# A graph network on one core: edge rows copied to PSUM by ScalarE in the first pass, row ends found tile by tile instead of by counting, and a longer ring of gathered rows

## The chip, the core and the metric

The kernel runs on one core of a Trainium2 chip. A time is the device time of one execution, in microseconds. The kernel before has the median, the lowest and the highest of three runs. The profile is one further execution, recorded by the hardware profiler. TensorE is called PE in the profile, VectorE DVE, ScalarE ACT, GpSimd POOL and SyncE SP.

## The reference

There are N = 6,250 nodes with 256 features and E = 100,000 edges, sorted by their destination `dst`; an edge also has 64 attributes. Two layers of message passing follow one another:

```
theta_x = (x[dst] - x[src]) @ theta_w.T + theta_b
phi_x   = x[src] @ phi_w.T + phi_b
x = layernorm(x + where(isfinite(m), m, 0)),  m = segment_max(relu(theta_x + phi_x), dst)

hv = x @ W_in + b_in
for W, b in ((W_u0, b_u0), (W_u1, b_u1)):
    msg = segment_max(relu(concat(hv[src], edge_attr) @ W + b), dst)
    hv  = where(has_in, msg + hv, hv)          # has_in: the node has an incoming edge
x = layernorm(x + relu(hv @ W_ro + b_ro))
```

All data are 32-bit floats. The relu and the terms of the destination don't depend on the choice of the edge, so they can be applied after the maximum: for the first layer the kernel needs the segment maximum of `x[src] @ (phi - theta)` alone, and for the other two rounds that of `hv[src] @ W[:256] + edge_attr @ W[256:]`.

## The kernel before

**Three passes.** `sweep(r)` runs three times, r = 0 for the first layer and r = 1, 2 for the two rounds of the second. Each pass reads a table in device memory, `table[r]`, with one row of 256 numbers a node: `table[0]` is `x @ (phi - theta)`, made in the prologue; pass 0 writes `table[1]` and pass 1 writes `table[2]`, a tile of 128 nodes at a time. There are 49 such tiles.

**Edges, blocks and steps.** The edges are laid out in reverse order of `dst`, in 14 blocks: 13 of 128 x 56 edges and a last of 128 x 54. Partition p of a block holds 56 consecutive edges. A step takes one edge of each partition, so a pass has 782 steps. Eight steps make a group (`K`).

**One step.** POOL gathers the 128 rows of the step's sources by an indirect DMA into `run`, a ring of groups (`sources`, line 790). It is issued `AHEAD` = 16 steps before the step, and the ring has four groups. DVE then keeps a running maximum along each partition (line 1043): the new value is `max(min(previous, lim), row)`, where `lim` is very low at the first edge of a node, so that the maximum starts anew there. The result replaces the gathered row. In passes 1 and 2 PE first multiplies the edge attributes of two steps (`pair`, line 825, into one of three PSUM buffers of the tag `he`, two pairs ahead), and DVE adds the gathered rows of both steps to it (line 1030). In pass 0 DVE takes the rows from SBUF as they were gathered. Forty steps of pass 0, the first two of each of the first 20 groups, are "raw": their rows are gathered from `x` itself, before the table is complete, then transposed and multiplied on PE (`raw_turn`, `raw_pair`).

**Behind the steps.** When a group is done SP stores it to `S[r]` (line 1051, 1 MB). At the end of a block `over_lanes` carries maxima over from partition to partition: PE transposes the last column, DVE scans it, PE transposes back, and ACT copies the result to `cs` (line 857).

**Node tiles.** `node(t, g, b)` puts the work of a tile of 128 nodes at slots, numbers of steps. At slot g POOL gathers the row of each node's last edge from S into `m` (line 870), which waits for the stores of S made so far. At b - 3 and b - 2 the maxima carried into the tile's partitions are picked by a matmul (`picks`, `carried`). In pass 0 follow `first_a` to `first_g`, from b to b + 9: the maximum with the carried one, adding theta of the node (from `h_sb`), relu times `has` on ACT (line 909), adding x, layernorm, two transposes (line 760), a copy by ACT (line 762), a product with `wcat` (line 768), the row for `table[1]` (line 926) and `h_sb`. In passes 1 and 2, `next_a` (lines 931 and 932) to `next_d` or `last_g` do the like with the next weights.

**Theta.** In pass 0, `theta(x)` of one tile each eight steps is made from a transposed copy of x, loaded by SP (lines 894, 897, 900).

**Counting.** The position of a node's last edge (`end_i`) and whether it has one (`has`) come from a count of edges by node, made in pass 0: `count(c)`, 98 times, one group each three steps from slot 28. DVE builds one-hot rows of the low 7 bits (`ol`, line 710) and of the tile number (`oh`, line 716), and PE adds up their products (line 721). At slots 322 and 323 `ends_a` and `ends_b` sum the counts. So no node tile of pass 0 starts before slot 324 (`begin`), which is in the sixth block.

**What sets the order.** The schedule is by hand. The loop over steps issues, for each step, a gather for 16 steps later, the pair two pairs ahead, DVE's work, the store, and then the tasks that `at(slot, ...)` has put there. Each engine works through its instructions in just this order, and waits on semaphores for operands and for free buffers. `node`'s slots are chosen at the end of `sweep`: b is at least `gap` slots (6, 4 and 6 in the three passes) after the tile before, and about 20 slots after the end of the last block that holds edges of the tile. `ahead` and `sources_next` gather the first 24 steps of the next pass while the present one ends.

A branch in `gnn_kernel` leads to `any_order`, for edges that are not sorted or lie otherwise than the blocks expect. It isn't taken with these inputs.

Of the kernel before, what the change touches and what calls it, by code (L numbers as in the profile page):

```python
# [8 lines left out]
F32 = mybir.dt.float32  # L9
# [14 lines left out]
K = 8  # L24
# [24 lines left out]
AHEAD = 2 * K  # L49
# [15 lines left out]
WIDE = max(sum(a <= b <= z for a, z in SPAN) for b in range(NB))  # L65

# [7 lines left out]
def gather_raw(nc, x, x_sb, s_r, i):  # L74

    nc.gpsimd.indirect_dma_start(out=x_sb[:, i, :], out_offset=None, in_=x,
                                 in_offset=bass.IndirectOffsetOnAxis(ap=s_r[:, i:i + 1], axis=0))
# [382 lines left out]
def gnn_kernel(  # L460
# [13 lines left out]
    above = const.tile([P, P], F32)  # L474
    nc.vector.tensor_scalar(above, jmp, 0.0, None, OP.is_gt)
# [4 lines left out]
    col = const.tile([P, P], BF16)  # L480
    nc.vector.tensor_copy(col, col_i)
# [22 lines left out]
    wd = const.tile([P, 2, D], F32)  # L504
    wt = const.tile([P, 2, D], F32)
# [6 lines left out]
    lo = const.tile([P, FS], BF16)  # L512
    hi = const.tile([P, FS], BF16)
    with tc.manual_schedule(), tc.tile_pool(name="pro", bufs=2) as pro, \
# [6 lines left out]
        for i in range(SOON):  # L521
            gather_raw(nc, x, x_sb, s_r, i)
        zero = pro.tile([1, D], F32, name="zero", bufs=1)
# [14 lines left out]
        def check():  # L538
# [15 lines left out]
            alike = BLOCKS.count(BLOCKS[0])  # L554
# [9 lines left out]
            nc.vector.tensor_scalar(bits, d_s, P - 1, None, OP.bitwise_and)  # L564
            nc.vector.tensor_copy(lo, bits)
            nc.vector.tensor_scalar(bits, d_s, 7, None, OP.arith_shift_right)
            nc.vector.tensor_copy(hi, bits)
# [29 lines left out]
def in_order(ctx: ExitStack, tc: tile.TileContext, g):  # L597
# [9 lines left out]
    table, ident, above, every, col, col_f = (g[n] for n in ("table", "ident", "above", "every", "col", "col_f"))  # L607
    whole, lim, lo, hi, s_s, fd, pd, ld, nd = (g[n] for n in ("whole", "lim", "lo", "hi", "s_s", "fd", "pd", "ld", "nd"))
    heT, xTn, xn, out = (g[n] for n in ("heT", "xTn", "xn", "out"))
    s_e, head, x, x_sb, wd, s_r = (g[n] for n in ("s_e", "head", "x", "x_sb", "wd", "s_r"))  # L610
    part = g["part"]
# [6 lines left out]
    has = one.tile([P, NT], F32, name="has")  # L618
# [3 lines left out]
    ones = one.tile([P, NT], F32, name="ones")  # L622
    nc.vector.memset(ones, 1.0)
# [18 lines left out]
    wcat = one.tile([P, 2, 2 * D], F32, name="wcat")  # L642
    nc.scalar.dma_start(wcat[:, :, :D], g["w_in"].rearrange("(k p) f -> p k f", p=P))
    winT = weight(g["w_inT"], "winT")
    wu0 = weight(g["w_u0"][:D, :], "wu0")
# [50 lines left out]
    hist = psum.tile([P, 512], F32, tag="v", name="hist", bufs=1)  # L696

    none = one.tile([P, NT], BF16, name="none")
    nc.vector.memset(none, 0.0)
    half = (NG + 1) // 2  # L700
    low = []
    for i in range(2):
        low.append(psum.tile([P, 512], F32, tag="he", name="low", bufs=3))
        n = min(half * K, FS - i * half * K)
        nc.scalar.copy(low[i][:, :n], lo[:, i * half * K:i * half * K + n])

    def count(c):
        k = min(K, FS - c * K)
        ol = work.tile([P, K, P], BF16, name="ol", bufs=1)
        nc.vector.tensor_tensor(ol[:, :k, :], col.unsqueeze(1).to_broadcast([P, k, P]),  # L710
                                low[c // half][:, c % half * K:c % half * K + k].unsqueeze(2).to_broadcast([P, k, P]), OP.is_equal)
        b = max(i for i in range(NB) if FIRST[i] <= c * K)
        tiles = [t for t in range(NT) if SPAN[t][0] <= b <= SPAN[t][1]]
        t0, w = tiles[0], len(tiles)
        oh = work.tile([P, K, WIDE], BF16, name="oh", bufs=1)
        nc.vector.tensor_tensor(oh[:, :k, :w], col[:, t0:t0 + w].unsqueeze(1).to_broadcast([P, k, w]),  # L716
                                hi[:, c * K:c * K + k].unsqueeze(2).to_broadcast([P, k, w]), OP.is_equal)
        if c == 0:
            nc.tensor.matmul(hist[:, :NT], ol[:, 0, :], none, start=True, stop=False)
        for j in range(k):  # L720
            nc.tensor.matmul(hist[:, t0:t0 + w], ol[:, j, :], oh[:, j, :w], start=False,  # L721
                             stop=(c == NG - 1 and j == k - 1))

    cnt, incl, end = (one.tile([P, NT], F32, name=n) for n in ("cnt", "incl", "end"))
    sums = []

    def ends_a():
        nc.vector.tensor_copy(cnt, hist[:, :NT])
        ps = psum.tile([P, 512], F32, tag="pr", name="sums")
        nc.tensor.matmul(ps[:, :NT], above, cnt, start=True, stop=True)  # L730
        nc.tensor.matmul(ps[:, 64:64 + NT], every, cnt, start=True, stop=True)
        sums.append(ps)
        nc.vector.tensor_scalar(has, cnt, 0.0, None, OP.is_gt)

    def ends_b():
        lower, total = sums[0][:, :NT], sums[0][:, 64:64 + NT]
        nc.vector.tensor_tensor_scan(incl, ones, total, 0.0, OP.mult, OP.add)
        nc.vector.tensor_sub(end, total, incl)
        nc.vector.tensor_sub(end, end, lower)
        nc.vector.tensor_add(end, end, has)  # L740
        nc.vector.tensor_scalar(end, end, float(E - 2), 0.0, OP.add, OP.max)
        nc.vector.tensor_copy(end_i, end)
# [22 lines left out]
    def times(aT, w, n, tag="pr"):  # L765
        ps = psum.tile([P, 512], F32, tag=tag, name="prod", bufs=3 if tag == "he" else 2)
        for k in range(2):
            nc.tensor.matmul(ps[:, :n], aT[:, k, :], w[:, k, :], start=(k == 0), stop=(k == 1))  # L768
        return ps

    def sweep(r):
# [12 lines left out]
        def sources(s, r=r, runs=runs):  # L784
            if s % K == 0:
                runs[s // K] = work.tile([P, K, D], F32, name="run", bufs=4)
# [7 lines left out]
        def raw_turn(i):  # L794

            tp = psum.tile([P, 512], F32, tag="tp", name="tp")
            for q in range(4):
                nc.tensor.transpose(tp[:, q * P:(q + 1) * P], x_sb[:, 2 * i + q // 2, q % 2 * P:(q % 2 + 1) * P], ident)
            rT[i] = work.tile([P, K // 2, P], F32, tag="hT", name="rT", bufs=4)
            nc.scalar.copy(rT[i].rearrange("p k e -> p (k e)"), tp)  # L800

        def raw_pair(i):
            aT = rT.pop(i)
            hp[i * K // 2] = psum.tile([P, 512], F32, tag="pr", name="hp")
            for q in range(4):
                nc.tensor.matmul(hp[i * K // 2][:, q // 2 * D:(q // 2 + 1) * D], aT[:, q, :], wd[:, q % 2, :],
# [26 lines left out]
        def over_lanes(b, last):  # L833
# [18 lines left out]
            def back():  # L852
# [4 lines left out]
                nc.scalar.copy(cs[:, b % KEPT, :D], cp[:, :D])  # L857
# [4 lines left out]
        def node(t, g, b):  # L862
# [5 lines left out]
            def rows():  # L868
                o["m"] = work.tile([P, D], F32, name="m", bufs=7)
# [8 lines left out]
            def picks():  # L878
                o["pick"] = []
                for blk in range(SPAN[t][0], SPAN[t][1] + 1):  # L880
                    p = work.tile([P, P], F32, name="pick", bufs=4)
# [10 lines left out]
            def x_in():  # L892
                o["xT"] = work.tile([P, K // 2, P], F32, tag="hT", name="xT", bufs=4)[:, :2, :]
                nc.sync.dma_start(o["xT"], xTn[:, :, t * P:(t + 1) * P])

            def theta():
                o["h"] = times(o["xT"], th, D, tag="he")

            def theta_out():
# [219 lines left out]
```

## Time and profile before

| what | us |
|---|---|
| runs: median (lowest to highest of three) | 4056.26 (4050.23 to 4058.96) |
| profiled execution | 4011.58 |
| its span | 4009.8 |
| pass 0, first to last step on DVE | 99.1 to 1366.2 |
| pass 1 | 1395.1 to 2678.2 |
| pass 2 | 2700.2 to 3994.0 |
| busy: PE, DVE, ACT, POOL | 1862.9, 2118.4, 238.2, 2391.0 |
| mean granted clock of TensorE | 0.689 |

"Busy" is the time in which an engine works on an instruction; an engine that waits for a semaphore isn't busy. In a row of groups, the numbers are: line, engine and operation, output and inputs by their names, sizes, count; busy time in us and mean of one in ns; the idle time just before these instructions, with what ended most of it. In a row of waits they are: the engine, the tile and line that waited, what it waited for, the total in us, how often, and the longest. "Issue" means that nothing in the trace shows a wait; "remote" is a semaphore whose event can't be told.

### The profile page before, as it was taken

How to read it: one execution, taken by the hardware profiler on the slowest of the kernel's cores; microseconds unless marked ns; L12 is line 12 of the kernel's file. 1: busy time of each engine (PE TensorE's matmuls, PEld its weight loads, DVE VectorE, ACT ScalarE, POOL GpSimd, SP SyncE). 2: the span in 40 equal slices, each digit the busy share in tenths (PEclk: the TensorE clock that was granted, in tenths of full speed). 3: DMA queues.
4: the chain of work that ended last, by engine and by line, in shares of the span. 5: the costliest groups of instructions: out<-in, count | busy, mean ns of one | idle time of the engine just before them, and what ended most of it. 6: DMA issues, size and time to landing. Idle time of an engine off the chain costs nothing. (4 is left out here: it accounts for less than half of the span.)

```text
span 4009.8 us, 21650 instructions
## 1 busy us (share of the span) xinstructions
PE 1862.9 (46%) x4631; PEld 825.8 (21%) x4631; DVE 2118.4 (53%) x4750; ACT 238.2 (6%) x618; POOL 2391.0 (60%) x2500
## 2 busy tenths in 40 slices
PE   5552123545520255454545555545544454444555
PEld 4341111212210122221112211111222221111111
DVE  1476444545543365554455555545756655555555
ACT  1000000111100000000000000000000000000000
POOL 5456546665667656656565656565655556666663
PEclk8665555766555578777676777667877777777766
DMA  6456545554555566555555556555555555555554
GB/s 235 149 197 231 171 140 178 188 165 165 177 193 169 178 198 203 185 178 185 170 182 187 192 197 207 185 175 192 194 181 179 183 181 189 182 182 193 186 194 161
DMA packets 241821, 739.39 MB, mean 184 GB/s; under 512 B 52485, under 2 KB 95858, under 8 KB 204434
## 3 DMA queue, kind: packets, MB, share of 16 engines
q0 software_dynamic: 119664, 326.92, 27.6%
q1 hardware_dynamic: 69568, 337.85, 22.6%
q10 hardware_dynamic: 52450, 73.16, 5.6%
q14 instruction: 100, 0.82, 0.1%
q8 instruction: 39, 0.64, 0.1%
HBM read 404.56 MB, written 333.17 MB: 184 GB/s over the span
## 5 line engine op out<-in xcount | busy, mean ns | idle before, releaser
L790 POOL DMA_INDIRECT run<-table,s_s x2258 | 2163.4, 958 | 1254.2 <-issue 666.1
L825 PE MATMUL hp<-whe,hT 128*128 128x512 f32 x1564 | 1015.0, 746 | 823.7 <-DVE run L1043 487.2
L1043 DVE SCALAR_TENSOR_TENSOR run<-run,lim,hp 128x256 f32<-128x256 f32 x1573 | 753.8, 479 | 55.7 <-issue 9.1
L1030 DVE TENSOR_TENSOR hp<-hp,run 128x512 f32<-128x512 f32 x782 | 543.2, 695 | 377.7 <-remote 196.2
L825 PEld LDWEIGHTS hp<-whe,hT 128*128 128x128 f32 x1564 | 300.8, 224 | 1369.8 <-DVE run L1043 815.7
L1043 DVE SCALAR_TENSOR_TENSOR run<-run,lim 128x256 f32<-128x256 f32 x731 | 351.5, 481 | 148.7 <-remote 56.0
L870 POOL DMA_INDIRECT m<-S,end_i x147 | 141.4, 962 | 304.5 <-DMA S<-run 177.0
L889 PE MATMUL v<-cs,pick 128*128 128x256 f32 (+1 forms) x438 | 167.0, 501 | 164.3 <-issue 71.0
L768 PE MATMUL prod<-wcat,aT 128*128 128x512 f32 x196 | 172.1, 1029 | 56.9 <-issue 34.0
L931 DVE TENSOR_TENSOR m<-m,v 128x256 f32<-128x256 f32 x98 | 40.6, 414 | 296.6 <-remote 232.1
L710 DVE TENSOR_TENSOR ol<-col,low 128x1024 bf16<-128x1024 bf16 x98 | 118.9, 1213 | 118.3 <-remote 103.9
L721 PE MATMUL hist<-oh,ol 128*128 128x8 bf16 (+7 forms) x782 | 34.9, 167 | 289.2 <-DVE oh L716 210.6
L889 PEld LDWEIGHTS v<-cs,pick 128*128 128x128 f32 x438 | 102.2, 253 | 270.4 <-issue 213.6
L768 PE MATMUL prod<-wro,aT 128*128 128x256 f32 x196 | 80.0, 548 | 166.0 <-issue 94.9
L947 DVE TENSOR_TENSOR m<-prod,bro 128x256 f32<-128x256 f32 x49 | 20.8, 425 | 233.0 <-remote 66.4
L768 PE MATMUL prod<-wu,aT 128*128 128x256 f32 x196 | 69.2, 486 | 91.2 <-issue 68.7
L926 DVE TENSOR_TENSOR new<-prod,b 128x256 f32<-128x256 f32 x49 | 20.8, 424 | 165.5 <-PE prod L768 67.3
L760 PE MATMUL tp<-ident,x_sb 128*128 128x128 f32 x98 | 31.8, 425 | 153.8 <-DVE x_sb L755 76.4
L721 PEld LDWEIGHTS <-ol 128*128 128x128 bf16 x782 | 36.4, 104 | 315.0 <-DVE ol L710 225.7
L932 ACT ACTIVATE m<-m,has 128x256 f32<-128x256 f32 x98 | 49.7, 508 | 858.8 <-DVE m L931 381.9
L760 PE MATMUL tp<-ident,h_sb 128*128 128x128 f32 x196 | 48.9, 338 | 110.9 <-DVE h_sb L935 52.0
L762 ACT COPY aT<-tp 128x256 f32<-128x256 f32 x147 | 54.8, 373 | 699.3 <-remote 292.7
(131 smaller groups left out, 1389.9 us busy)
## 6 DMA issues: line engine op xcount, KB each, us to landing
S<-run SPq DMA_DIRECT2D x291, 1024.0 KB
hT<-in_heT ACTq DMA_DIRECT2D x196, 256.0 KB
run<-table,s_s POOLq DMA_INDIRECT x2258
table<-new ACTq DMA_DIRECT2D x98, 128.0 KB
xg<-in_xTn SPq DMA_DIRECT2D x7, 896.0 KB
xT<-in_xTn SPq DMA_DIRECT2D x49, 128.0 KB
x_sb<-in_xn SPq DMA_DIRECT2D x7, 896.0 KB
out<-new ACTq DMA_DIRECT2D x48, 128.0 KB
```

What stands on the lines that cost most here:

```text
L710: nc.vector.tensor_tensor(ol[:, :k, :], col.unsqueeze(1).to_broadcast([P, k, P]), low[c // half][:, c % half * K:c % half * K + k].unsquee ...
L721: nc.tensor.matmul(hist[:, t0:t0 + w], ol[:, j, :], oh[:, j, :w], start=False, stop=(c == NG - 1 and j == k - 1))
L760: nc.tensor.transpose(tp[:, k * P:(k + 1) * P], a[:, k * P:(k + 1) * P], ident)
L762: nc.scalar.copy(aT.rearrange("p k e -> p (k e)"), tp[:, :2 * P])
L768: nc.tensor.matmul(ps[:, :n], aT[:, k, :], w[:, k, :], start=(k == 0), stop=(k == 1))
L790: nc.gpsimd.indirect_dma_start(out=runs[s // K][:, s % K, :], out_offset=None, in_=table[r][:SPARE + 1, :] if early else table[r], in_offs ...
L825: nc.tensor.matmul(hp[i], hT[c][:, q, :], whe[r - 1].rearrange("p s f -> p (s f)"), start=True, stop=not early)
L870: i = nc.gpsimd.indirect_dma_start(out=o["m"], out_offset=None, in_=S_r[:P * (FIRST[SPAN[t][1]] + BLOCKS[SPAN[t][1]]), :], in_offset=bass. ...
L889: nc.tensor.matmul(o["v"][:, :N1], p, cs[:, blk % KEPT, :N1], start=(blk == SPAN[t][0]), stop=(blk == SPAN[t][1]))
L932: nc.scalar.activation(o["m"], o["m"], AF.Relu, scale=has[:, t:t + 1])
L1030: nc.vector.tensor_add(sums, sums, two)
L1043: nc.vector.scalar_tensor_tensor(cur, prev, lim[:, s:s + 1], row, OP.min, OP.max)
```

## The change

- `AHEAD` is 24 steps, and the ring of `run` has five groups. In passes 1 and 2 every sixth group takes the place of three weights, `wd`, `wt` and `wcat`, which only the prologue and pass 0 use and which now lie together in `first_w`.
- To find room, `m` has five buffers instead of seven, and `winT` and `wu0` are loaded into tiles of `hT`'s ring.
- The counting is gone, with its one-hots, `ends_a`, `ends_b` and `begin`. In its place, `ends(t)` finds the last edges of one tile twelve slots before they are gathered: for each block that the tile spans, two operations mark the partition whose run holds a node's last edge, a matmul picks that partition's list of destinations, and DVE counts along it. `keeps` takes the place of `has`: very high where a node has an edge and very low where not.
- Node tiles of pass 0 therefore start after the first block, 8 slots apart instead of 6.
- In pass 0 all rows reach DVE through PSUM: ACT copies each pair of steps from `run` to a PSUM buffer of the tag `he` (`bring`), two pairs ahead. Raw pairs use the same buffers.
- In pass 0, x of a tile is transposed on PE from `x_sb` instead of loaded transposed; theta stays in PSUM, with its bias added by a matmul with the identity; `x_sb` is loaded earlier, and raw rows lie in it in reverse order.
- `first_b` is two DVE operations, without ACT; `next_a` is one, and the relu of the carried maxima moves to the copy to `cs`. Later parts of a node come one to two slots earlier, and nodes start about 28 slots after the end of their block.

```diff
-AHEAD = 2 * K
+AHEAD = 3 * K
...
-    wd = const.tile([P, 2, D], F32)
-    wt = const.tile([P, 2, D], F32)
+    first_w = const.tile([P, K, D], F32)
+    wd, wt = first_w[:, 0:2, :], first_w[:, 2:4, :]
...
+    wcat = g["first_w"][:, 4:8, :].rearrange("p (k two) f -> p k (two f)", k=2)
     nc.scalar.dma_start(wcat[:, :, :D], g["w_in"].rearrange("(k p) f -> p k f", p=P))
-    winT = weight(g["w_inT"], "winT")
-    wu0 = weight(g["w_u0"][:D, :], "wu0")
+    winT, wu0 = (work.tile([P, K // 2, P], F32, tag="hT", name=n, bufs=4).rearrange("p (k h) f -> p k (h f)", k=2)
+                 for n in ("winT", "wu0"))
+    nc.scalar.dma_start(winT, g["w_inT"].rearrange("(k p) f -> p k f", p=P))
+    nc.scalar.dma_start(wu0, g["w_u0"][:D, :].rearrange("(k p) f -> p k f", p=P))
...
-    def count(c):
...
+    def ends(t):
+        b0, b1 = SPAN[t]
+        top = work.tile([P, NB], F32, name="top")
+        nc.vector.tensor_scalar(top[:, b0:b1 + 1], fn[:, 0, b0:b1 + 1], float(-P * t), None, OP.add)
+        ps = psum.tile([P, 512], F32, tag="tp", name="ends")
+        for b in range(b0, b1 + 1):
+            own = work.tile([P, P], F32, tag="pick", name="here", bufs=4)
+            nc.vector.tensor_scalar(own, col_f, fn[:, 1, b:b + 1], float(-P * t), OP.subtract, OP.is_gt)
+            nc.vector.scalar_tensor_tensor(own, col_f, top[:, b:b + 1], own, OP.is_le, OP.mult)
+            nc.tensor.matmul(ps[:, :BLOCKS[0] + 1], own, lane[:, b, :], start=b == b0, stop=b == b1)
+        found = work.tile([P, 2, BLOCKS[0]], F32, name="found")
+        num = work.tile([P, 2], F32, name="num")
+        for i, op in enumerate((OP.is_ge, OP.is_equal)):
+            nc.vector.scalar_tensor_tensor(found[:, i, :], ps[:, :BLOCKS[0]], n1[:, t:t + 1], every[:, :BLOCKS[0]], op,
+                                           OP.mult, accum_out=num[:, i:i + 1])
+        nc.vector.tensor_scalar(end_i[:, t:t + 1], ps[:, BLOCKS[0]:BLOCKS[0] + 1], num[:, 0:1], 0.0, OP.add, OP.max)
+        nc.vector.tensor_scalar(keeps[:, t:t + 1], num[:, 1:2], 0.0, 2.0 * BIG, OP.is_gt, OP.mult)
+        nc.vector.tensor_scalar(keeps[:, t:t + 1], keeps[:, t:t + 1], -BIG, None, OP.add)
...
+    def times(aT, w, n, more=None):
+        ps = psum.tile([P, 512], F32, tag="pr", name="prod")
         for k in range(2):
-            nc.tensor.matmul(ps[:, :n], aT[:, k, :], w[:, k, :], start=(k == 0), stop=(k == 1))
+            nc.tensor.matmul(ps[:, :n], aT[:, k, :], w[:, k, :], start=(k == 0), stop=(k == 1 and more is None))
+        if more is not None:
+            nc.tensor.matmul(ps[:, :n], ident, more, start=False, stop=True)
...
-                runs[s // K] = work.tile([P, K, D], F32, name="run", bufs=4)
+                spare = r > 0 and s // K % 6 == 3
+                runs[s // K] = g["first_w"] if spare else work.tile([P, K, D], F32, name="run", bufs=5)
...
+        def bring(i):
+            hp[i] = psum.tile([P, 512], F32, tag="he", name="hp", bufs=3)
+            if raw(2 * i) is None:
+                c, q = divmod(i, K // 2)
+                nc.scalar.copy(hp[i], runs[c][:, 2 * q:2 * q + 2, :].rearrange("p s f -> p (s f)"))
...
-                nc.scalar.copy(cs[:, b % KEPT, :D], cp[:, :D])
+                nc.scalar.activation(cs[:, b % KEPT, :D], cp[:, :D], AF.Copy if r == 0 else AF.Relu)
...
-                o["m"] = work.tile([P, D], F32, name="m", bufs=7)
+                o["m"] = work.tile([P, D], F32, name="m", bufs=5)
...
+            def x_turn():
+                o["xT"] = turned(x_sb[:, t, :])
 
             def theta():
-                o["h"] = times(o["xT"], th, D, tag="he")
-
-            def theta_out():
-                nc.vector.tensor_add(h_sb[:, t, :], o["h"][:, :D], tb)
+                o["h"] = times(o["xT"], th, D, more=tb)
...
-                nc.vector.tensor_add(o["m"], o["m"], h_sb[:, t, :])
-                nc.scalar.activation(o["m"], o["m"], AF.Relu, scale=has[:, t:t + 1])
-
-            def first_c():
-                nc.vector.tensor_add(o["m"], o["m"], x_sb[:, t, :])
+                nc.vector.scalar_tensor_tensor(o["m"], o["m"], keeps[:, t:t + 1], o["h"][:, :D], OP.min, OP.add)
+                nc.vector.scalar_tensor_tensor(o["m"], o["m"], 0.0, x_sb[:, t, :], OP.max, OP.add)
...
-                nc.vector.tensor_max(o["m"], o["m"], o["v"][:, :D])
-                nc.scalar.activation(o["m"], o["m"], AF.Relu, scale=has[:, t:t + 1])
+                nc.vector.scalar_tensor_tensor(o["m"], o["m"], keeps[:, t:t + 1], o["v"][:, :D], OP.min, OP.max)
...
-                at(8 * i + 8, x_in)
-                at(8 * i + 20, theta)
-                at(8 * i + 21, theta_out)
+                at(max(2, g_ - 12), ends, t)
+                at(b - 6, x_turn)
+                at(b - 4, theta)
             at(b - 3, picks)
             at(b - 2, carried)
             if r == 0:
-                for i, f in ((0, first_a), (1, first_b), (3, first_c), (4, first_d), (6, first_e), (7, first_f),
-                             (9, first_g)):
+                for i, f in ((0, first_a), (1, first_b), (2, first_d), (4, first_e), (5, first_f), (7, first_g)):
                     at(b + i, f)
             else:
-                for i, f in ((0, next_a), (2, next_b), (3, next_c)):
+                for i, f in ((0, next_a), (0, next_b), (1, next_c)):
                     at(b + i, f)
-                for i, f in ((5, next_d),) if r == 1 else ((5, last_d), (6, last_e), (8, last_f), (9, last_g)):
+                for i, f in ((3, next_d),) if r == 1 else ((3, last_d), (4, last_e), (6, last_f), (7, last_g)):
...
-            for c in range(NG):
-                at(3 * c + 28, count, c)
-            begin = 3 * NG + 30
...
-        gap = (6, 4, 6)[r]
+            for i in reversed(range(NT // PART)):
+                last = RAW - 1 - i * PART
+                at(8 * (last // 2 - 2) + 2 if last > 5 else 2, lambda i=i: nc.sync.dma_start(
+                    x_sb[:, i * PART:(i + 1) * PART, :], xn[:, i * PART:(i + 1) * PART, :]))
+        gap = (8, 4, 6)[r]
         b = 0
         for t in reversed(range(NT)):
-            e = max(FIRST[SPAN[t][1]] + BLOCKS[SPAN[t][1]], begin)
+            e = FIRST[SPAN[t][1]] + BLOCKS[SPAN[t][1]]
...
+                else:
+                    if s == 0:
+                        bring(1)
+                    if s + 4 < FS:
+                        bring(s // 2 + 2)
```

## The prediction

> **What bounds the kernel now.** I read the windows first, one for each pass over the edges, and two for the stages of pass 0 (counting; then its node tiles). Columns are named in the first line.
>
> ```profile
> core 0: us, PE busy (x) PEld busy (x) DVE busy (x) ACT busy (x) POOL busy (x), PEclk, DMA share, GB/s
> 99.10:1366.20 1267.10, 471.40 (x1721) 253.59 (x1719) 644.65 (x1564) 95.32 (x253) 766.88 (x786) 0.58 0.53 177
> 1395.10:2678.20 1283.10, 662.76 (x1317) 256.55 (x1315) 692.52 (x1422) 53.25 (x136) 771.61 (x813) 0.73 0.57 188
> 2700.20:3994.00 1293.80, 642.65 (x1317) 253.25 (x1315) 754.22 (x1662) 67.05 (x184) 767.13 (x808) 0.76 0.57 186
> 99.10:624.00 524.90, 187.80 (x1222) 138.61 (x1221) 299.29 (x603) 15.23 (x36) 286.98 (x298) 0.56 0.54 180
> 624.00:1138.00 514.00, 252.48 (x449) 102.59 (x447) 253.59 (x752) 72.00 (x192) 324.08 (x330) 0.62 0.52 170
> ```
>
> No engine is full anywhere, so the order of waits decides. The gathers come next, POOL's waits over the whole run and its gather rows in pass 0 and in pass 1:
>
> ```profile
> POOL run L790 <- issue: 680.2, 2144, 4.9
> POOL run L790 <- DVE run L1043: 257.3, 46, 22.6
> POOL m L870 <- DMA S<-run: 177.0, 28, 14.3
> POOL run L790 <- DVE hp L1030: 101.5, 20, 20.6
> ...
> POOL run L790 <- DVE oh L716: 67.6, 8, 14.9
> ```
> ```profile
> L790 POOL DMA_INDIRECT run<-table,s_s x732 | 713.9, 975 | 376.9 <-issue 220.4 <-DVE oh L716 67.6 <-DVE run L1043 57.7
> ```
> ```profile
> L790 POOL DMA_INDIRECT run<-table,s_s x757 | 719.0, 950 | 431.5 <-issue 224.9 <-DVE hp L1030 85.0 <-DVE h_sb L935 59.9
> ```
>
> A gather costs 0.95 us and 0.30 us to the next issue (220.4/732): 1.256 us for 128 rows. Pass 0 issues 742 gathers of rows and 49 of node tiles: 791 x 1.256 = 993 us, against 1267. The other 270 us are POOL waiting for a free group of the ring, that is for DVE, or for S. In pass 1 the same sum is 813 x 1.254 = 1,020 us, and again some 260 us are waits. There, though, rows lie landed 5 to 40 us before DVE takes them: POOL's waits are the consequence, and DVE with PE the cause. The timeline in a block of pass 1 shows it (start, duration, engine; idle time before and its releaser in brackets):
>
> ```profile
> 2145.04 1.12 PE L825 MATMUL hp<-whe,hT 128*128 128x512 f32 x2 [0.52 <-DVE run L1043]
> ...
> 2152.68 0.70 DVE L1030 TENSOR_TENSOR hp<-hp,run 128x512 f32<-128x512 f32 x1 [6.05 <-remote]
> ...
> 2154.47 2.08 PE L825 MATMUL hp<-whe,hT 128*128 128x512 f32 x2 [6.66 <-issue]
> ...
> 2158.28 0.70 DVE L1030 TENSOR_TENSOR hp<-hp,run 128x512 f32<-128x512 f32 x1 [3.87 <-remote]
> ```
> ```profile
> 2112.50:2150.00 37.50, 27.02 (x69) 10.30 (x67) 32.32 (x67) 2.97 (x8) 25.91 (x28) 1.00 0.76 256
> 2150.00:2204.60 54.60, 22.44 (x31) 8.87 (x32) 18.35 (x38) 1.39 (x3) 30.21 (x32) 0.50 0.46 147
> ```
>
> At a granted clock of 1.00 DVE does a pair of steps each 1.64 us; then, once a block, for some 50 us at 0.50, an add each 5.6 us, released late by PE. A block's 56 steps thus take 87 to 112 us once nodes run in it. Over such blocks PE sustains 403 to 412 columns of f32 a us (columns of all recorded matmuls over the block's time).
>
> **The change, part by part.** It is summed against the profiled execution (4011.58 us; its span is 4009.8); the runs' median, 4056.26, stands 1.1% above.
>
> *Counting goes.* Pass 0 loses, 98 times, two one-hot builds on DVE (1.213 us at L710, about 0.19 at L716: 137 us) and eight small matmuls, and DVE's waits for them (104 us ahead of L710). More than the busy time, the order matters: no node tile could start before slot 324, as all counts had to be in; in the counting stage POOL stalled 147 us over six blocks (524.9 less 298 x 1.27), 67.6 us of it on L716.
>
> *`ends` comes.* For each of 49 node tiles DVE makes two 128x128 operations for each block spanned (73 in all, 1.5 a tile, at 0.298 us, the row of L882), two 128x56 with a sum (put at 0.25 each) and four of one column (0.151, the row of L904): 2.0 us. PE gets about three records of 57 columns. DVE waits for these, in order: about 1 us, from 0.5 (two records at L721's 167 ns and a semaphore) to 5.6 (a slow stretch).
>
> *Nodes spread.* They now begin after the first block: 0, 4, 6, 6, 6, 5, 5, 4, 3, 3, 2, 2, 1, 1 in the 14 blocks, one after the end, every eighth step at the densest. Before it was 8 to 10 in five blocks, every sixth step. A node's own work on DVE was about 3.9 us (with theta's add); two adds and theta's (3 x 0.42) become two operations at 0.484: 3.6. With `ends` 5.6 us. Its waits: in the node stage DVE idled 139.2 us ahead of 42 adds at L926, 3.3 us each; with 1 for `ends` and 0.3 for the rest, 4.6. So a node costs DVE 10.2 us, and 56 steps 27 us (0.479 each).
>
> *Rows through ScalarE.* 371 copies of 128x512 into PSUM; the nearest rows are the other way round, 588 ns (L579) and 586 (L800). I take 0.587: 218 us, and ACT goes from 95 to some 310 us of pass 0. Two pairs ahead and with three PSUM buffers, a copy has about two pairs, 5 us at POOL's pace, to be done; it is hidden. Bounds: 0.4 to 1 us each makes 150 to 370 us, still hidden. ACT is in order: a copy that waits for rows holds aT's and h_sb's copies behind it, and PE's products and DVE's L926 wait for those. Rows come each 2.5 us a pair, so this holds a node up by 0 to 2.5 us; within the 4.6.
>
> *What the row's new place saves POOL.* 975 ns against 950: 25 x 742 = 18 us. The Trainium skill ("SBUF — State Buffer", Who interferes with whom) says that a DVE instruction with two SBUF inputs and a GpSimd one that reads SBUF block each other entirely. The running maximum of pass 0 holds DVE 28% of the time (351.5 of 1267), so a gather would lose 0.28 x 0.24 = 0.067 us, 50 us in all. The row shows less than half of it. I take the row; by the rule pass 0 would end some 25 us earlier than my sum.
>
> *Ring and lead.* 24 steps ahead over five groups (six later). In passes 1 and 2 I cost it at nothing: rows are early already, and what hides it is DVE with PE. Node rows get 5 buffers rather than 7: in pass 1 the sixth gather of a block waits until DVE has done the first, which leaves a lead of 16 steps, today's. Bound: 0 to 20 us a pass lost. The node's relu on ACT goes, one DVE operation replaces the maximum; 0 to 10 us a pass won.
>
> *Moved.* xT's 49 loads leave SP's queue; x is transposed on PE (two records and one ACT copy, 0.37 us), theta's bias becomes two matmuls; 20 PE records and 5,041 columns a node (counted in the code) instead of 16 and 4,876. The other moves (x_sb's seven loads earlier on SP, where they stand ahead of the first groups' stores to S, which five groups of ring cover; `new`'s stores, behind the copies on ACT, needed only in pass 1; two weights in hT's ring; three iotas in the prologue, beside POOL's 25.1 us wait ahead of its first gather) cost nothing unless the wait at slot 12 for the weights, about 18 us today, grows.
>
> **Sum for pass 0.** Per block the longer of POOL, (56+n) x 1.256, and DVE, 27 + 10.2n. Block 0 holds the weights' wait (93.6 us today; a longer lead takes about 13): 80. Block 1: 70 (seven raw pairs are not gathered then). Blocks 2 to 4: DVE, 88 each. 5 and 6: 78. 7: 75. Then POOL: 74, 74, 73, 73, 72, 69. Sum 1,080, against 1,267: 187 us less. The rest unchanged: 4011.6 - 187 = 3,825; at the runs' level x 1.011 = 3,867.
>
> **The clock speaks against this.** Row: 5.6 us for a pair (1,024 columns) in a slow stretch, against 1.12 recorded at full clock. Rule: the skill ("TensorE: Matmul & The Clock Gate", What's actually happening) puts an idle PE at half clock, after a window of about 3.4 us; with counting gone, PE idles more. By the rule a node takes 5,041/1,024 x 1.12 = 5.5 us warm and 11.0 cold, just under the 11.3 that POOL needs for eight steps and the node's gather: all hidden, and 1,080 stands. By the row it is 27.6 us, were every node in a slow stretch. Before's node stage lies between: about 44,000 columns in 99 to 109 us, 365 to 448 a us, so 12 us a node. I take that; it is inside the 14.0 of DVE (10.2 and eight steps).
>
> **Rivals.**
> - *PE's slow stretches eat most of it.* Blocks 1 to 6, with 32 nodes, need 187,000 columns (raw pairs and block ends in). At 443 a us they take 422 us, hidden in my 490; at 330 they take 567, 77 more; at 303, 127 more. Gain 110 to 60: 3,945 to 3,995. For it: 0.56 granted while counting, at little load. Chance 0.18.
> - *The ring frees passes 1 and 2.* Their POOL waits are 260 us each; were a fifth to a half of it on the path, 105 to 265 us more: 3,600 to 3,760. Against: the rows' early landing. Chance 0.12.
> - *Slower.* The same PE in the same blocks, but near the slow rate, as thinly spread nodes find it cold each time. It decides from 187,000 columns in 490 + 187 = 677 us: 276 a us. At 230 they take 813: 136 us more, about 4,195. Against: never so low on average in any stage with nodes. Chance 0.11.
> - *It doesn't matter*, since nodes only move and gathers wait elsewhere in pass 0: within 0.2%. It would need 187 us of new waits exactly. Chance 0.02.
>
> **How the numbers follow.** The main case has 0.57, its own range 3,790 to 3,935 (port rule, all waits hidden, down to POOL's 1,000 us; PE a little late). Range for 8 in 10: 3,730 (some help from the ring) to 3,995 (the whole first rival). Faster by over 0.2% (8 us, about what a measurement of this kernel can tell from none): 0.57 + 0.18 + 0.12 = 0.87; same 0.02; slower 0.11.
>
> **What would show it.** Right: pass 0's steps last about 1,080 us, POOL's gathers there fall to about 950 ns with under 100 us of waits, the waits at L710 and L716 are gone, blocks 2 to 4 are the longest, ACT is busy about 310 us, and passes 1 and 2 stay within 30 us of 1,283 and 1,294. Wrong: DVE waits for PE in `ends` or L926 over 5 us a node; ACT's copies land after DVE asks for them; or passes 1 and 2 move by more than 30 us.

## The result, and the profile after

The changed kernel takes 4391.67 us (median of four runs, 4383.66 to 4414.01) against 4055.7 (four runs) for the kernel before: 1.0837 times as long, with a 95% interval of 1.0802 to 1.0872. The forecast was 3,867, 0.953 times. The profiled execution has a span of 4412.2 us. These are its three passes in the view of windows (the columns are named in the first line):

```profile
core 0: us, PE busy (x) PEld busy (x) DVE busy (x) ACT busy (x) POOL busy (x), PEclk, DMA share, GB/s
100.70:1460.20 1359.50, 468.17 (x1270) 292.19 (x1269) 591.66 (x1849) 287.65 (x623) 745.12 (x786) 0.63 0.47 159
1488.40:2933.30 1444.90, 635.97 (x1317) 259.40 (x1315) 698.77 (x1422) 29.00 (x88) 769.06 (x813) 0.74 0.51 167
2955.40:4396.70 1441.30, 675.55 (x1317) 266.21 (x1315) 761.60 (x1662) 42.60 (x136) 764.79 (x808) 0.73 0.50 167
```

Pass 0 takes 92 us more than before (1359.5 against 1267.1), pass 1 162 and pass 2 148. The busy times show no reason: DVE works 53 us less in pass 0 and 6 to 7 us more in the others, POOL 22 us less in pass 0 and within 3 us of before in the others, and PE as long in sum. All of the loss is waiting. In passes 1 and 2 neither a gather nor a matmul was added.

The first reading is from DVE's idle time, group by group in pass 0 (shapes, count, busy us and mean ns, then the idle time ahead and its releasers):

```profile
L717 DVE SCALAR_TENSOR_TENSOR found<-ends,n,every 128x56 f32<-128x56 f32 x98 | 23.2, 274 | 70.8 <-remote 34.3 <-PE ends L713 29.1 <-issue 6.6
...
L906 DVE TENSOR_TENSOR new<-prod,b 128x256 f32<-128x256 f32 x48 | 20.4, 425 | 384.2 <-remote 154.3 <-PE prod L747 122.2 <-issue 100.3
...
L887 DVE TENSOR_SCALAR no<-v 128x1 f32<-128x1 f32 x48 | 7.4, 155 | 99.0 <-remote 62.8 <-issue 27.5 <-PE v L876 7.5
```

For a node of pass 0 DVE waits 384.2/48 = 8.0 us ahead of the add that takes its product, 2.1 for the carried maxima and 1.4 in `ends`: 11.5 us, where the sum had 4.6. Where the trace names the one that ended the wait, it is PE; for most of the time it doesn't. The second reading is from the timeline of a block of pass 1 (start, duration, engine, operation; idle time ahead in brackets):

```profile
2036.05 0.94 POOL L857 DMA_INDIRECT m<-S,end_i  x1 [18.19 <-DMA S<-run]
...
2060.51 0.69 PE L739 MATMUL tp<-ident,h_sb 128*128 128x128 f32 x2 [5.30 <-DVE h_sb L914]
...
2070.06 0.37 ACT L741 COPY aT<-tp 128x256 f32<-128x256 f32 x1 [37.34 <-issue]
2070.49 2.07 PE L747 MATMUL prod<-wu,aT 128*128 128x256 f32 x4 [9.29 <-issue]
...
2081.21 0.42 DVE L922 TENSOR_TENSOR new<-prod,bu 128x256 f32<-128x256 f32 x1 [18.34 <-issue]
...
2121.58 0.66 PE L739 MATMUL tp<-ident,h_sb 128*128 128x128 f32 x2 [6.80 <-DVE h_sb L914]
...
2122.33 0.37 ACT L741 COPY aT<-tp 128x256 f32<-128x256 f32 x1 [12.67 <-PE tp L739]
...
2128.33 0.94 POOL L772 DMA_INDIRECT first_w<-table,s_s  x1 [17.56 <-DVE h_sb L914]
```

Two transposes of 0.69 us, recorded from 2060.51, let ScalarE begin only at 2070.06, 8.9 us after their recorded end; the product begun at 2070.49 reaches DVE at 2081.21. At 2121.58 the same transposes, with nearly the same recorded length (0.66 us), release ScalarE in 0.1 us. What goes with the difference in this trace is POOL. It paused for 18.19 us up to 2036.05, gathered without a break until about 2110, and paused again for 17.56 us up to 2128.33. PE answers late from some 20 us after a pause until some us into the next.

Such a stretch can be counted: idle times of DVE over 2.4 us that lie less than 13 us apart, taken together where they hold 15 us or more. In passes 1 and 2 the kernel before has 30 of them, 42 us long in the median, 967 us of idle in all; the changed kernel has 29 of 58 us, 1,264 us of idle. The 297 us between are nearly the 309 us that the two passes lost.

### The profile page after: what moved, and what is told of

Its sections match the earlier page's. It is cut to its first block, busy times and chain, and to the rows that moved or that the text cites. A ratio compares the mean times of both kernels' runs of the same rounds, so it can differ in the third digit from the quotient of the medians.

```text
span 4412.2 us, 22105 instructions
## 1 busy us (share of the span) xinstructions
PE 1866.9 (42%) x4186; PEld 881.7 (20%) x4186; DVE 2078.4 (47%) x5034; ACT 380.5 (9%) x889; POOL 2363.7 (54%) x2503
## 5 line engine op out<-in xcount | busy, mean ns | idle before, releaser
L772 POOL DMA_INDIRECT run<-table,s_s x2002 | 1896.0, 947 | 1097.1 <-issue 575.9
L812 PE MATMUL hp<-whe,hT 128*128 128x512 f32 x1564 | 982.7, 725 | 346.3 <-DVE run L1014 182.5
L1014 DVE SCALAR_TENSOR_TENSOR run<-run,lim,hp 128x256 f32<-128x256 f32 x2024 | 966.7, 478 | 183.4 <-remote 49.9
L1002 DVE TENSOR_TENSOR hp<-hp,run 128x512 f32<-128x512 f32 x654 | 454.4, 695 | 85.1 <-remote 35.5
L772 POOL DMA_INDIRECT first_w<-table,s_s x256 | 242.7, 948 | 149.1 <-issue 63.3
L747 PE MATMUL prod<-first_w,aT 128*128 128x256 f32 (+1 forms) x392 | 241.6, 764 | 131.5 <-ACT aT L741 89.2
L789 ACT COPY hp<-run 128x512 f32<-128x512 f32 x371 | 219.2, 592 | 447.7 <-issue 243.0
L911 DVE SCALAR_TENSOR_TENSOR m<-m,keeps,v 128x256 f32<-128x256 f32 x98 | 46.9, 478 | 398.0 <-remote 306.1
L739 PEld LDWEIGHTS tp<-ident,h_sb 128*128 128x128 f32 x196 | 24.4, 175 | 721.7 <-issue 633.8
L747 PEld LDWEIGHTS prod<-first_w,aT 128*128 128x128 f32 x392 | 114.6, 313 | 204.7 <-ACT aT L741 97.7
```

The source lines that it names most:

```text
L739: nc.tensor.transpose(tp[:, k * P:(k + 1) * P], a[:, k * P:(k + 1) * P], ident)
L772: nc.gpsimd.indirect_dma_start(out=runs[s // K][:, s % K, :], out_offset=None, in_=table[r][:SPARE + 1, :] if early else table[r], in_offs ...
L789: nc.scalar.copy(hp[i], runs[c][:, 2 * q:2 * q + 2, :].rearrange("p s f -> p (s f)"))
L812: nc.tensor.matmul(hp[i], hT[c][:, q, :], whe[r - 1].rearrange("p s f -> p (s f)"), start=True, stop=not early)
L911: nc.vector.scalar_tensor_tensor(o["m"], o["m"], keeps[:, t:t + 1], o["v"][:, :D], OP.min, OP.max)
L1002: nc.vector.tensor_add(sums, sums, runs[c][:, j:j + 2, :].rearrange("p s f -> p (s f)"))
```

## Experiments

The experiments fell on five chips, which are of two kinds. On three, kind A (chip A in the expectations), the kernel before takes 4,002 to 4,056 us; on two, kind B, 3,214. The measurement above and the profiles of before and after are of kind A. Every ratio is to the kernel before on the same chip. "Changed" is the changed kernel.

**Lead, place, PE's load, ScalarE's copies (kind A).**

```diff
x1_lead16: changed, with
+AHEAD = 2 * K
x2_nodes20: changed, with
+            b = max(b + (gap if b < FS else 3), e + 4, min(e + 2 * K + 4, FS + 4))
+            node(t, max(e, b - 2 * K - 4), b)
x3_pair_bf16: changed, with
+            nc.tensor.matmul(hp[i], hT[c][:, q, :].bitcast(BF16)[:, 1::2], whe[r - 1]....bitcast(BF16)[:, 1::2], ...
x4_no_copy: changed, with (in bring)
+                hp[i] = runs[c][:, 2 * q:2 * q + 2, :].rearrange("p s f -> p (s f)")
-                nc.scalar.copy(hp[i], ...)
```

> The changed kernel with 16 steps of lead instead of 24; the ring keeps five and six groups. With it a node's work starts about 20 slots after its block's end, as before, instead of 28. Theory A (PE has slow stretches in which each of its instructions costs some 3 us, and the new place of the node tiles puts their many small matmuls into these stretches): passes 1 and 2 come back to about 1,290 us each, the whole to 4,080 to 4,150. Theory B (the lead itself hurts, through node rows' five buffers and POOL's order): the same, 4,080 to 4,150. Theory C (the shortened node, with its parts one or two slots earlier, hurts): no change, 4,350 to 4,420.

> The changed kernel with 24 steps of lead, but node tiles placed as for 16 (about 20 slots after their block's end, their rows gathered 20 slots ahead). Theory A: place is all, so as with 16 steps of lead, 4,080 to 4,150. Theory B: the lead is still 24, no change, 4,350 to 4,420. Theory C: no change, 4,350 to 4,420.

> The changed kernel with the matmul of each pair of steps in passes 1 and 2 fed with the upper halves of its 32-bit numbers as bfloat16; the edge attributes and their weights are thus cut to 8 bits of mantissa.[...] Theory A, where the slow stretches come from sustained work of PE: they grow rare, passes 1 and 2 fall by 150 to 300 us each, to 4,000 or below. Theory A, where they come from an idle PE: no gain or a loss, 4,350 to 4,600. Theory B: no change, 4,350 to 4,420.

> The changed kernel with pass 0's rows read by VectorE from SBUF, as before, without ScalarE's 371 copies. Theory A and B: pass 0 within 20 us, since ScalarE isn't the bound; POOL's gathers 25 ns longer; 4,370 to 4,420. Rival, ScalarE's copies hold the nodes' own copies: pass 0 falls by 60 to 100 us, 4,290 to 4,330.

Measured: x1 4522.33 us, ratio 1.128 (1.1221 to 1.1339); x2 4284.9, 1.0695 (1.0631 to 1.0759); x3 4212.51, 1.0517 (1.0458 to 1.0577); x4 4358.15, 1.0874 (1.0813 to 1.0934). Place is worth about 0.015, so theory A is no more than a part. Less lead in the longer ring is worse still, with passes 1 and 2 at 1,475 and 1,501 us: against all three theories. With pairs in bfloat16, whose recorded matmuls take 221 us of pass 1 instead of 476, 0.03 is won: the stretches are fewer (22 instead of 29) but hardly shorter (55 us). Without ScalarE's copies the whole is no faster by its ratio, and DVE still waits 374 us ahead of line 906. Pass 0 of that trace lasts 1,314 us, against 1,359 and, in y1 below, 1,345 with the copies; some 18 us of this is the faster chip (4,002 against 4,056 us before), so a gain of 15 to 30 us isn't excluded.

**The node's form and slots.** On kind B came first:

```diff
x5_slots: changed, with the slots of before
+                for i, f in ((0, first_a), (1, first_b), (4, first_d), (6, first_e), (7, first_f), (9, first_g)):
+                for i, f in ((0, next_a), (2, next_b), (3, next_c)):
+                for i, f in ((5, next_d),) if r == 1 else ((5, last_d), (6, last_e), (8, last_f), (9, last_g)):
x6_slots_nodes20: x5 and x2 together
x7_times_bf16: changed, with next_c's two operands as .bitcast(BF16)[:, 1::2]
x8_before_node: before, with next_a, the relu in cs and the slots of passes 1 and 2 from the changed kernel
```

> The changed kernel with the parts of a node at the slots of before, counted from its start b (0, 2, 3, 5 and on; in pass 0 as before too). Theory C (with its parts drawn together, PE stands waiting for VectorE and ScalarE inside each node, falls to the slow state, and pays for each of the node's matmuls there): passes 1 and 2 fall from about 1,440 to 1,300 each, pass 0 by 50 or more; ratio to before 0.98 to 1.02. Theory A (place of the nodes against their block): no change, 1.07 to 1.09. Theory D (a node's new operations themselves, whatever their slots): no change, 1.07 to 1.09.

> The same with the node tiles about 20 slots after their block's end, as before. Theory C: within 0.02 of the kernel with the old slots alone. Theories A and C together: 0.02 to 0.04 below it, since placing nodes so was worth 0.014 with the new slots. Theory D: 1.05 to 1.07, as with the place alone.

> The changed kernel with the last product of a node in passes 1 and 2 (two of its five to six matmuls) fed with the upper halves of its numbers as bfloat16[...]. If a matmul in the slow stretch costs by its passes (about 1.4 us each, whatever its columns): some 8 us less per node, for those 3 of 4 to 5 nodes of a block that fall in the stretch: passes 1 and 2 fall by 200 to 300 us together, ratio 1.01 to 1.04. If the stretch is made of waits between engines: within 30 us, 1.075 to 1.09.

> The kernel before with the changed kernel's node in passes 1 and 2 alone: next_a as one operation without ScalarE, relu in the copy to cs, and the parts at slots 0, 0, 1, 3 and on. Lead, ring and place stay as before. Theories C and D: passes 1 and 2 rise by 100 to 150 us each, ratio 1.05 to 1.075. Theory A: within 0.01 of before.

Measured on kind B, where before takes 3214.43: x5 3166.26, 0.9846 (0.983 to 0.9863); x6 3166.1, 0.9851 (0.9835 to 0.9868); x7 3181.39, 0.9892 (0.9876 to 0.9909); x8 3216.52, 1.0002 (0.9993 to 1.0011). These tell nothing between the theories, as the loss isn't there at all. They show what this chip does otherwise. The windows of x5's three passes, and its waits of POOL and DVE:

```profile
76.50:1066.20 989.70, 436.47 (x1270) 269.17 (x1268) 595.64 (x1849) 291.54 (x623) 741.50 (x783) 0.68 0.65 219
1093.20:2107.60 1014.40, 660.43 (x1317) 263.94 (x1315) 698.21 (x1422) 29.04 (x88) 766.38 (x810) 0.82 0.72 237
2131.20:3149.30 1018.10, 663.86 (x1317) 267.61 (x1315) 762.30 (x1663) 42.69 (x136) 767.61 (x808) 0.83 0.71 236
```
```profile
POOL run L772 <- issue: 552.4, 1813, 0.3
...
POOL run L772 <- DVE run L1014: 15.2, 50, 0.3
```
```profile
DVE hp L1002 <- DMA run<-table,s_s: 351.8, 194, 4.5
```

POOL pauses for 0.3 us between gathers and for more than 1.5 us only once in passes 1 and 2. It gathers one step each 1.25 us from end to end, and all passes stand at its floor, 990 to 1,018 us; DVE waits for rows. PE isn't late: the same transposes, in this trace,

```profile
1639.74 0.69 PE L739 MATMUL tp<-ident,h_sb 128*128 128x128 f32 x2
1640.52 0.37 ACT L741 COPY aT<-tp 128x256 f32<-128x256 f32 x1 [37.59 <-PE tp L739]
```

release ScalarE in 0.09 us. Gathers cost the same on both kinds (0.95 us and 0.30). What differs is how late PE answers, not what the records of its matmuls say.

The same question on kind A:

```diff
y1_again: changed
y2_slots: as x5
y3_before_node: as x8
y4_filled: changed, with, ahead of a node's transposes (5) and of each of its products (4),
+            nc.tensor.matmul(ps, ident.bitcast(BF16)[:, 1::2], whe[0]....bitcast(BF16)[:, 1::2], start=True, stop=True)
```

> The changed kernel as it is, beside the three that follow. Two chips have been seen: one on which the kernel before takes about 4,000 us (chip A) and one on which it takes 3,214 (chip B). On chip A 1.08 of before; on chip B, where gathers bind all passes and PE isn't late, 0.985 to 0.99.

> The changed kernel with a node's parts at the slots of before. On chip A: theory C (parts drawn together leave PE standing, its clock falls, and on this chip a matmul then costs several us), 0.98 to 1.03; theories A and D, 1.07 to 1.09. On chip B 0.985 again.

> The kernel before with the changed node, form and slots, in passes 1 and 2. On chip A: theories C and D, 1.04 to 1.075; theory A, within 0.01 of before. On chip B 1.000 again.

> The changed kernel with nine short matmuls in bfloat16 (128x512, whose results are overwritten) in each node, five ahead of the transposes and four ahead of the product, where PE otherwise stands waiting. On chip A: if an idle PE is what brings the slow stretches on, fewer of them, 0.98 to 1.05; if sustained work brings them on, or if the clock stays low, each costs another 1.4 us or so in a stretch: 1.10 to 1.16. On chip B: 0.985 to 1.00, since PE has room.

Measured: y1 4400.55, 1.085 (1.0797 to 1.0902), as before; y2 4354.81, 1.0709 (1.0643 to 1.0775); y3 4063.66, 1.0032 (1.001 to 1.0053); y4 4560.67, 1.1251 (1.1193 to 1.1308). The changed node alone costs 0.003, and the old slots in the changed kernel win 0.014: theories C and D fall as the main cause. Nine short matmuls a node, put where PE stood waiting, make it worse and leave 31 stretches of 55 us, so filling PE in this way doesn't keep the stretches away.

**The ring.** I then sorted a node's transposes of passes 1 and 2 (those for which ScalarE stood waiting) by the time since POOL's last pause of over 1.5 us, and counted those whose copy began over 2 us after their recorded end:

| | POOL pauses | 0 to 10 us after | 10 to 20 us | over 20 us |
|---|---|---|---|---|
| before, kind A | 1 of 22 | 0 of 38 | 7 of 23 | 14 of 14 |
| changed, kind A | 3 of 42 | 0 of 11 | 5 of 5 | 39 of 39 |
| x3 (pairs in bfloat16), kind A | 2 of 30 | 0 of 6 | 0 of 6 | 32 of 55 |
| x1 (lead 16, longer ring), kind A | 6 of 33 | 0 of 7 | 0 of 26 | 32 of 32 |
| x5, kind B | none | none | 0 of 1 | 0 of 96 |

On kind A, PE answers promptly while POOL stands and shortly after, and late once POOL has gathered for 20 us on end; with less work on PE (x3), from 30 us on. POOL stops only when the ring is full (or a node's rows wait for S). Theory R: a longer ring lets POOL go on longer, and so makes each late stretch longer.

```diff
z2_ring4, w1_ring4: changed, with
+AHEAD = 2 * K
+                runs[s // K] = work.tile([P, K, D], F32, name="run", bufs=4)
z4_before_ring5, w2_before_ring5: before, with wd, wt and wcat in first_w, and
+                spare = r > 0 and s // K % 5 == 3
+                runs[s // K] = g["first_w"] if spare else work.tile([P, K, D], F32, name="run", bufs=4)
z3_before_ring3: before, with bufs=3, AHEAD = K, and nodes placed by 2 * K
z1_spaced: changed, with behind each gather of passes 1 and 2
+                nc.gpsimd.iota(space, pattern=[[1, 64]], base=0, channel_multiplier=0)
```

> The changed kernel with the ring of before: four groups in all passes, 16 steps ahead. Theory R (on chip A, PE answers late while POOL gathers without a pause, and a longer ring lets POOL go on for longer before it must wait): passes 1 and 2 return to 1,280 to 1,330 us each, ratio to before 0.99 to 1.04. If the ring isn't it: 1.07 to 1.13, as with 16 steps of lead in the long ring (1.128). On chip B: 0.985 to 1.00.

> The kernel before with one group more in passes 1 and 2, which takes the room of the three weights as in the changed kernel; lead 16 and all else as before. Theory R: the slow stretches grow by 8 steps' gathers, some 10 us a block, so 100 to 140 us a pass, ratio 1.03 to 1.07. If the ring isn't it: 0.995 to 1.005. On chip B: 1.00.

> The kernel before with a ring of three groups and 8 steps of lead, nodes where they were. Theory R: shorter stretches, passes 1 and 2 lose 50 to 130 us each, 0.93 to 0.98, unless VectorE now waits for rows. If the ring isn't it: 1.00 to 1.06, since less lead covers less. On chip B: 1.01 to 1.06.

> The changed kernel with one small operation of POOL (a ramp of 64 numbers a partition, used by nobody) behind each gather of passes 1 and 2, so that gathers come some 0.2 to 0.5 us further apart. Theory R: PE is late less often, passes 1 and 2 fall to 1,300 to 1,380 us, ratio 1.02 to 1.06. If POOL's pace only follows: no gain, 1.08 to 1.12. On chip B, where gathers bind: 1.05 to 1.25.

These four fell on kind B, where PE isn't late: z2 3214.72, 1.0004 (0.9995 to 1.0012); z4 3208.02, 0.9983 (0.9976 to 0.9989); z3 3252.61, 1.0123 (1.0106 to 1.014); z1 3288.27, 1.0232 (1.0215 to 1.0249). There a longer ring is a small gain, a shorter one a loss, and spacing the gathers only lengthens them. The first two were run again, and fell on kind A:

> Once more the changed kernel with the ring of before (four groups, 16 steps ahead). On chip A, theory R: POOL must pause sooner, the slow stretches shrink from 60 us to 45, passes 1 and 2 return to 1,280 to 1,330 us each, ratio 0.99 to 1.04. If the ring isn't it: 1.07 to 1.13. On chip B 1.000, as measured.

> Once more the kernel before with one group more in passes 1 and 2. On chip A, theory R: slow stretches some 10 us longer in each block, ratio 1.03 to 1.07; if the ring only hurts together with the longer lead, 0.995 to 1.01. On chip B 0.998, as measured.

w1 took 4109.54 against 4056.26 us: 1.013 (1.0066 to 1.0193). w2 took 4238.03 against 4027.46: 1.0539 (1.0473 to 1.0604). The windows of their passes, w1 first:

```profile
103.10:1409.40 1306.30, 464.51 (x1270) 291.20 (x1268) 590.25 (x1849) 287.90 (x623) 744.10 (x786) 0.62 0.49 166
1435.60:2727.60 1292.00, 637.63 (x1317) 255.37 (x1315) 700.63 (x1422) 29.00 (x88) 769.16 (x813) 0.75 0.56 187
2749.70:4085.40 1335.70, 672.71 (x1317) 264.83 (x1315) 763.83 (x1662) 42.65 (x136) 764.69 (x808) 0.74 0.54 180
```
```profile
98.40:1341.00 1242.60, 472.73 (x1721) 252.82 (x1719) 643.89 (x1564) 95.40 (x253) 771.53 (x789) 0.57 0.55 180
1370.60:2738.10 1367.50, 651.83 (x1317) 256.42 (x1315) 690.47 (x1422) 53.25 (x136) 771.70 (x813) 0.73 0.54 176
2760.30:4204.20 1443.90, 664.55 (x1317) 263.82 (x1315) 756.29 (x1663) 67.06 (x184) 768.08 (x808) 0.72 0.51 167
```

Without the longer ring, passes 1 and 2 of the changed kernel return from 1,445 and 1,441 us to 1,292 and 1,336, and its late stretches from 58 us to 43, nearly those of before. With one group more and nothing else, the same passes of the kernel before rise from 1,283 and 1,294 to 1,368 and 1,444, and its stretches from 42 to 54 us, with 1,231 us of idle instead of 967. w1's setting of 16 steps differs from x1's only in the ring: 1.013 against 1.128. This holds in every trace of kind A: with four groups (before, y3, w1) the stretches are 42 to 43 us long in the median, with the longer ring (the changed kernel, y1, y2, y4, x1 to x4, w2) 54 to 63, whatever the lead, the place or the slots. Nor is it the place of the extra group among the weights: in pass 0, where no group lies there, x1 takes 1,378 us and w1 1,306. So it is shown from both sides that the longer ring makes the stretches longer. That it does so through POOL's unbroken gathering, as theory R has it, fits most of the nodes counted and is in part argued.

What isn't settled is what in POOL's unbroken gathering delays PE, the gathers themselves or something that goes with them: z1, which was to tell it, ran on kind B alone. In w2's trace ten of 32 transposes are late within a pause too, and two of 18 in the 10 us after. Node by node, with all slots the same, 17 nodes that were prompt in the kernel before are late in w2, and ten of these stand outside the rule of the table; from w1 to x1 it is six of 23. It also stays open why, in the longer ring, 16 steps of lead cost 0.043 more than 24 (1.128 against 1.085). Nor was the changed kernel itself run on kind B; its nearest there is x7, with one product cut to bfloat16, at 0.989.

No kernel run here was faster than before on kind A. On kind B, x5 and x6 are the fastest, 1.5% under the kernel before.

## Why the prediction was wrong, point by point

- **The step that failed in passes 1 and 2 is "Ring and lead": "In passes 1 and 2 I cost it at nothing: rows are early already, and what hides it is DVE with PE."** The first half holds: in passes 1 and 2 of the changed kernel rows land over 4 us before DVE takes them. The second was taken for a cause that stands by itself. It does not: how long PE is late depends on the ring. The longer ring with its lead costs 0.072 of the 0.085 (1.085 for the changed kernel again, 1.013 without them), and one group more in the kernel before alone costs 0.054. The bounds of 0 to 20 us a pass lost held no such term; what was lost is about 150 us a pass. I had called POOL's 260 us of waits a pass mere consequences; by the table above PE's recovery goes with them.
- **The term for a node's waits in pass 0 was too small:** 11.5 us measured for 4.6. With it the sum's own rule, 27 + 17.1n for 3.6 + 2.0 + 11.5 us a node, gives 130 us for blocks of six nodes, where 88 was written; they took 100 to 120. Pass 0 took 1,359.5 instead of 1,080: blocks 1 to 6 took 631 for 490, and blocks 7 to 13, put down to POOL at 510 in sum, took 634. With the old ring in w1 pass 0 still takes 1,306, against 1,267, so the ring is not all of it there.
- **Under this term lay a misreading of the kernel before.** "About 44,000 columns" a block in its node stage, "so 12 us a node", is nine nodes at 4,876 columns. But 4,876 holds the counting and theta, which were over or nearly so by then. The rows of that stage (624 to 1138 us) have these matmuls, and 25 more of 128 columns:

```profile
L768 PE MATMUL prod<-wcat,aT 128*128 128x512 f32 x176 | 153.2, 1021 | 54.3 <-issue 31.9 <-ACT aT L762 22.3
L889 PE MATMUL v<-cs,pick 128*128 128x258 f32 x124 | 52.1, 539 | 101.3 <-DVE pick L882 44.7 <-issue 41.3 <-DVE m L912 10.2
L760 PE MATMUL tp<-ident,x_sb 128*128 128x128 f32 x88 | 28.3, 422 | 96.6 <-DVE x_sb L755 48.4 <-DVE no L904 30.4 <-issue 9.0
L768 PE MATMUL prod<-wt,xT 128*128 128x256 f32 x36 | 16.3, 606 | 0.0
```

  That is about 146,000 columns in 514 us, 283 a us and not 365 to 448. At this rate a node of 5,041 columns takes 17.8 us, more than the 14.0 that DVE had, and blocks 1 to 6 with their 187,000 columns take 661 us. They took 631. By the prediction's own measure, then, most of the gain in pass 0 was not there to be had.
- **The rest of the costs held.** Copies: 0.591 us (0.587 forecast), ACT 288 us busy (some 310), and taking them away changed nothing clear of noise (1.0874 against 1.0837 and 1.085). Gathers in pass 0: 948 ns (950). `ends`: 351 and 291 ns for the two 128x128 operations, 274 for the 128x56, where 298 and 250 were assumed. One sum is off: by the port rule pass 0 would end 50 - 18 = 32 us earlier, not 25; nothing hung on it.
- **The rival that ended slower** named PE in blocks 1 to 6 of pass 0, and put break-even at 276 columns a us. Those blocks took 631 us for 187,000 columns, 296 a us: near break-even, but pass 0 counts for 92 of the 402 us of span. The larger part lies in passes 1 and 2, which no rival on that side had. The rival "the ring frees passes 1 and 2" had the right part of the change and the wrong sign.
- **The clock rule.** In the slow stretches the record shows 0.5, as the Trainium skill ("TensorE: Matmul & The Clock Gate", What's actually happening) has it for an engine that idles. But two transposes at 0.50 answer in 0.09 us both on kind B (1639.74) and in the changed kernel itself (2121.58), and filling PE (y4) left the stretches as they were. The half clock goes with the stretches and doesn't make them by itself.
- **The aim of the change** can be seen on kind B: with PE prompt, gathers bind, and x5's pass 0 takes 990 us, POOL's floor, against 1,023 in x8, where pass 0 is as before. With the new slots it is less: pass 0 takes 1,008 us in x7, whose pass 0 is the changed kernel's, and 1,020 without the longer ring and its lead (z2, in all 1.0004). Without these two the rest of the change, the end of the counting with it, made the kernel faster on neither kind (w1 1.013). The forecast of 187 us rested on waits of kind A that the change did not remove.

## What to carry to other kernels

A buffer that fills is also a brake: before a longer ring is costed at nothing because the consumer never starves, ask what the producer's pauses do for the engines that the consumer waits for. Where results come much later than their records end, find out on what the lateness depends (here: the time since another engine last paused) before it is treated as a fixed rate. And a tuned kernel may be tuned to a kind of chip: run both on more than one before a few per cent are believed.

## What was not expected of the hardware

- The same kernel takes 3,214 us on two chips and 4,002 to 4,056 on the others, with equal gathers (0.95 us) and, at the same granted clock, equal recorded transposes (0.69 us for two). On the slower kind PE's results come some 9 us after the recorded end of two transposes, 10.7 us after the start of a product, 5.6 us a pair, in stretches of 42 to 63 us in the median of a trace.
- In such a stretch columns count for little: two transposes of 128 columns took 9.5 us (2060.51 to 2070.06), four records of 256 columns 10.7 (2070.49 to 2081.21), a pair with two records of 512 columns 5.6.
- A running maximum with both operands in SBUF cost each gather some 25 ns: 975 in the kernel before against 948 in the changed one, and 969 again in x4, which brings the two operands back. That is a good third of the 67 ns that the prediction worked out for full blocking.
